# Two transformer blocks with cross attention on one core: weight loads queued one by one, and three value steps moved before the first unit

## The chip, the cores and the metric

The kernel runs on one core of a Trainium2 chip. The metric is the device time of one execution in microseconds (us). The median of three runs of the kernel before is 3282.65 us (3281.64 to 3282.78). The core has a matrix engine (TensorE, PE), a vector engine (VectorE, DVE), a scalar engine (ScalarE, ACT), a general engine (GpSimd, POOL) and a synchronising engine (SyncE, SP), which here issues nearly all DMA transfers.[...]

## The reference

Two layers of the same form are applied to `x` (4 batch items, 512 rows, 320 columns, float32). Each layer has self attention, cross attention to a context of 1601 rows and 192 columns, and a gated feed-forward part; 20 heads of 16 columns.

```python
def _attn(x, ctx, wq, wk, wv, wo, bo, heads):
    q, k, v = ...            # x @ wq, ctx @ wk, ctx @ wv, split into heads
    sim = jnp.einsum('bhid,bhjd->bhij', q, k) * scale
    a = jax.nn.softmax(sim, axis=-1)
    out = jnp.einsum('bhij,bhjd->bhid', a, v)
    ...
    return out @ wo + bo

h1 = _ln(x, n1_g, n1_b)
x = _attn(h1, h1, q1, k1, v1, o1_w, o1_b, heads) + x
h2 = _ln(x, n2_g, n2_b)
x = _attn(h2, context, q2, k2, v2, o2_w, o2_b, heads) + x
h3 = _ln(x, n3_g, n3_b)
proj = h3 @ ff_w1 + ff_b1
a, g = jnp.split(proj, 2, axis=-1)
x = a * jax.nn.gelu(g, approximate=False) @ ff_w2 + ff_b2 + x
```

## The kernel before

**Units.** The work is cut into units (class `Unit`, L206). A self or cross unit is one group of 4 heads of one batch item; there are 5 groups and 4 items, so 20 self units and then 20 cross units per layer. A feed-forward unit is one batch item. The loop at L1179 runs over all units in order. Unit numbers in this document count from 0 within a layer.

**One attention unit** (`main`, L870). The keys are taken in chunks of 128: 4 chunks in a self unit, 13 in a cross unit. For each chunk the scores of the four heads are made on PE (L878), in two half-steps of two heads. ScalarE takes the exponential (L884), and one chunk later the values are summed on PE (L898). From the second chunk on, ScalarE copies the sum (L914) and GpSimd adds it (L915). In a unit that the feed-forward part follows, VectorE does both.

**The maxima.** The exponential needs the maximum of each score row before it starts. So while a unit runs, the full score rows of a later unit are made once more on PE (L717, and L732 for the last 65 keys of a cross unit) and VectorE reduces them (L725). `max_end` (L768) transposes the negated maxima on VectorE (L772) and sends them by eight small DMAs (L779) from the tile `turned` into spare rows of the query tile `q`, where the score matmul subtracts them. It is called for the next unit at the third chunk from the end (L949), in a self unit at the second of four. The next unit's first score waits for those transfers.

**How the maxima are spread.** `giver` (L1094) hands out, at each half-step, one pair of maxima matmuls for the units one and two ahead. Where time presses it adds whole rounds of four ("extra"). Between two extra rounds, one piece of planned work is run if any is ready (L944 to L947).

**The planner.** All other work stands in seven chains (L261): norm, context, projections of queries and keys (`add_proj`, L545), values (`add_values`, L652), division of the sums, output projection (`add_finish`, L784). Each piece has a cost and a due round. A round is one half-step. `pick` (L295) takes the ready piece with the earliest due round; `pace` (L309) works out the cost per round that the due rounds ask for; `tick` adds it to a credit between -2 and 4; `steps` (L331) runs pieces while the credit covers a share of their cost. `until` forces a chain where its result is needed at once. Light pieces (statistics, normalisation, division) run one or two per chunk.

**Queues.** Loads, the small transfers of the maxima, and the transfers `aT<-o` of finished units (L817) are all issued by SP, in the order of the program, and share its queue. Only the eight transfers of unit 0's maxima are divided over SP, ScalarE and GpSimd.

**The start** (L1145 to L1177). The first item of `x` and the first self weights are loaded; the queries and keys of units 0 and 1, the queries of unit 2, the maxima of unit 0 and half of the value steps are worked out; `max_end(first)` sends the maxima. Then the other three items of `x`, the first output weights, the cross weights and the feed-forward weights are loaded in one block (L1170 to L1174), one key projection runs, and the loop over the units begins.

**Later loads.** `after(u)` (L1061) runs when a unit's work on an item is complete. When it is the last item of a part, `after` loads the weights of the same part for the next layer, and the next output weights, at once. For the feed-forward part that is at the start of layer 2's self units.

Of the kernel before, what the change touches and what calls it, by code (L numbers as in the profile page):

```python
# [20 lines left out]
L = 2  # L21
# [38 lines left out]
def kernel(ctx: ExitStack, tc: tile.TileContext, x, context, ws, out):  # L60
# [69 lines left out]


    xs = [const.tile([P, NQ, D], F32, name=f"x{b}") for b in range(B)]

    def load_x(b):
        src = x[b].rearrange("(c p) d -> p c d", p=P)
        for t in range(NQ) if b == 0 else (slice(NQ),):
            dma(out=xs[b][:, t], in_=src[:, t])


    wq1, wk1, wv1, wq2 = (wpool.tile([P, 3, D], F32, name=n) for n in ("wq1", "wk1", "wv1", "wq2"))  # L140
# [8 lines left out]
    brow = [wpool.tile([P, D], F32, name=f"brow{i}") for i in range(2)]  # L149
    lng = [wpool.tile([P, 3], F32, name=f"lng{i}") for i in range(3)]  # L150
    lnb = [wpool.tile([P, 3], F32, name=f"lnb{i}") for i in range(3)]

    def load_rows(t, w, chunks):
        for k, at, n in chunks:
            dma(out=t[:n, k, :], in_=w[at : at + n, :])
# [15 lines left out]
    def load_norm(l, i):  # L171
        for t, v in ((lng[i], ws[l][f"n{i + 1}_g"]), (lnb[i], ws[l][f"n{i + 1}_b"])):
            load_columns(t, v, FK if i == 2 else DK)
            if i == 2:
                for half in range(2):
                    load_columns(t[half * REST :], v, [(2, 2 * P, REST)])
# [7 lines left out]
    def load_out(l, name):  # L184
        load_rows(wo, ws[l][name], DK)

    def load_cross(l):
        load_norm(l, 1)
        load_rows(wq2, ws[l]["q2"], DK)
        load_rows(wk2, ws[l]["k2"], CK)  # L190
        load_rows(wv2, ws[l]["v2"], CK)

    def load_ff(l):
        load_norm(l, 2)
        with nc.allow_non_contiguous_dma(reason="a vector's elements go to partitions"):
            dma(out=b1, in_=ws[l]["ff_b1"].rearrange("(c p) -> p c", p=P))
        load_rows(w1, ws[l]["ff_w1"], FK)
        for half in range(2):
            dma(
                out=w1r[half * REST : (half + 1) * REST, :],  # L200
                in_=ws[l]["ff_w1"][2 * P :, half * FF : (half + 1) * FF],
            )
        dma(out=w2, in_=ws[l]["ff_w2"].rearrange("(c p) f -> p c f", p=P))


    class Unit:  # L206
# [96 lines left out]
    def run(chain):  # L303
        costs, _, ready, _, f = chains[chain].popleft()
        assert ready(), chain
        f()
        clock["credit"] -= sum(costs)
# [80 lines left out]
    def add_norm(l, b, i, put, done, due):  # L388
        xb = xs[b]
        s = {}  # L390

        def stats(t):
            if t == 0:
                hn_used.append(b)
                s["mv"] = two.tile([P, NQ, 2], F32, tag="mv", name="mv")
            st = three.tile([P, 6], F32, tag="st6", name="st6")
            nc.vector.bn_stats(st, xb[:, t, :])
            nc.vector.bn_aggr(s["mv"][:, t, :], st)

        def root():  # L400
            s["rstd"] = inverse_root(s["mv"][:, :, 1])
            s["round"] = clock["round"]

        def normalise(t):
            if t == 0:
                s["hn"] = one.tile([P, NQ, D + REST], F32, tag="hn", name="hn")

            for to, at, n in ((0, 0, D), (D, D - REST, REST))[: 1 + i // 2]:
                nc.vector.tensor_scalar(
                    s["hn"][:, t, to : to + n], xb[:, t, at : at + n],  # L410
                    s["mv"][:, t, 0:1], s["rstd"][:, t : t + 1], ALU.subtract, ALU.mult,
                )
            s["round"] = clock["round"]

        def turn(k, at, n):
            if k == 0:
                s["hT"] = two.tile([P, 3, N], F32, tag="hT", name="hT")
                readers.append(done)
            ps = step_bank([P, N], "hps")
            n += REST if n == REST else 0  # L420
            for t in range(NQ):
                nc.tensor.transpose(ps[:n, t * P : (t + 1) * P], s["hn"][:, t, at : at + n], ident)  # L422
            if start["on"] and k == 1:
                nc.vector.tensor_scalar(
                    s["hT"][:n, k, :], ps[:n, :],
                    lng[i][:n, k : k + 1], lnb[i][:n, k : k + 1], ALU.mult, ALU.add,
                )
            else:
                nc.scalar.activation(
                    s["hT"][:n, k, :], ps[:n, :], AF.Identity,  # L430
                    bias=lnb[i][:n, k : k + 1], scale=lng[i][:n, k : k + 1],
                )
            for t in ((0,), (1,), (2, 3))[k]:

                nc.gpsimd.tensor_tensor(xb[:, t, :], xb[:, t, :], brow[(3 * l + i) % 2], ALU.add)
            if k == 2:
                hn_used.pop()
                put(s["hT"])

        for t in range(NQ):  # L440
            add(
                "norm", LIGHT, lambda t=t: stats(t), due - 22 + t,
                (lambda: stage[b] == 3 * l + i and not hn_used) if t == 0 else yes,
            )
        add("norm", LIGHT, root, due - 18)
        for t in range(NQ):
            add(
                "norm", LIGHT, lambda t=t: normalise(t), due - 13 + t, yes,
                (lambda: clock["round"] >= s["round"] + 4) if t == 0 else yes,
            )  # L450
        for k, at, n in (DK if i < 2 else FK + [(2, 2 * P, REST)]):
            add(
                "norm", 0.58, lambda k=k, at=at, n=n: turn(k, at, n), due - 6 + 2 * k,
                may_overwrite if k == 0 else yes, lambda: clock["round"] >= s["round"] + 1,
            )
# [312 lines left out]
    def max_end(u):  # L768

        turned = two.tile([P, SLOT], F32, tag="turned", name="turned")  # L770

        nc.vector.transpose(turned, u.nm)  # L772
        for half in range(2):
            slots = u.q[half * GD : (half + 1) * GD, :].rearrange("(j s) n -> s j n", s=SLOT)[AUG[2 * half]]
            for i in range(P // SLOT):
                rows = slice(i * SLOT + half * 2 * NQ, i * SLOT + (half + 1) * 2 * NQ)

                queue = (nc.sync, nc.scalar, nc.gpsimd, nc.sync)[i] if start["on"] else nc.sync
                queue.dma_start(  # L779
                    out=slots.rearrange("j (t r) -> j t r", t=NQ)[:, :, i * SLOT : (i + 1) * SLOT],  # L780
                    in_=turned[rows, :],
                )
# [87 lines left out]
    def main(u, give, nxt):  # L870
# [48 lines left out]
        for c in range(u.nch):  # L919
            extra = []  # L920
            if last:

                round_of(
                    [
                        lambda j=j, ring=ring: score(c, j, *ring)
                        for j, ring in zip(range(HG), ((ps_st, "st"), (ps_m, "m")) * 2)
                    ],
                    [],
                )
                tick()  # L930
            else:
                for odd in range(2):
                    if odd:
                        tick()
                    pair, rounds = give(2 * c + odd)
                    extra += rounds
                    round_of([lambda j=j: score(c, j) for j in ((2, 3) if odd else (0, 1))], pair)
            u.scored = c + 1
            flush()
            late.append(lambda c=c: values(c))  # L940
            steps(None, 1 if extra or c == u.nch - 1 else 2)

            start["quad"] = True
            for i, e in enumerate(extra):  # L944
                if i and next_cost() is not None:
                    run(pick())
                round_of([], e)  # L947
            start["quad"] = False
            if not last and c == u.nch - 3:  # L949
                max_reduce(nxt)  # L950
                max_end(nxt)

# [106 lines left out]
    def after(u):  # L1061

        stage[u.b] += 1
        if u.b == B - 1:
            load_bias(u.l, ("self", "cross", "ff").index(u.kind) + 2)
        if u.b == B - 1 and u.l + 1 < L:
            {"self": load_self, "cross": load_cross, "ff": load_ff}[u.kind](u.l + 1)
        if u.b == B - 1 and u.kind == "self":
            load_out(u.l, "o2_w")
        if u.b == B - 1 and u.kind == "cross" and u.l + 1 < L:  # L1070
            load_out(u.l + 1, "o1_w")

    def left(v):
        return sum(map(len, v.pairs))
# [92 lines left out]
    run("values")  # L1167
    max_reduce(first)
    max_end(first)
    for b in range(1, B):  # L1170
        load_x(b)
    load_out(0, "o1_w")
    load_cross(0)
    load_ff(0)  # L1174
    start["on"] = start["both"] = False
    run("proj")
    clock["credit"] = 0.0  # L1177

    for i, u in enumerate(units):  # L1179
# [42 lines left out]
```

## Time and profile before

| what | value |
|---|---|
| median of 3 runs | 3282.65 us |
| the profiled execution | 3282.7 us |
| its span, first to last instruction | 3280.9 us |
| PE busy | 3225.2 us (98%) |
| DVE, ACT, POOL busy | 2093.1, 2030.4, 1524.9 us |
| mean granted PE clock | 0.995 of full speed |
| DMA, mean over the span | 16 GB/s |
| share of PE in the chain that ended last | 89% |

The profile records one execution. A row of the timeline gives start and length in us, the engine, the line of the kernel, the operation, what is written and read, and in brackets how long the engine stood idle before it and what ended that. "SPq" is SP issuing transfers. The window rows give the busy time of each engine within a stretch, then the granted clock, the mean share of the 16 DMA engines in use and GB/s. The rows that carry the argument stand in the prediction.

### The profile page before, as it was taken

What the parts mean: (1) busy time and instruction counts of PE and PEld (TensorE: products, weight loads), DVE (VectorE), ACT (ScalarE), POOL (GpSimd) and SP (SyncE); (2) the same over time, 40 slices, a digit from 0 to 9 for tenths busy, and PEclk for the clock granted to TensorE, in tenths of its full rate; (3) what the DMA queues carried; (4) which work ended last, traced back from release to release, by engine and by line L of the source; (5) the groups of instructions that cost most, each with busy time, mean ns of one, the idle gap of its engine ahead of it and who ended that gap; (6) DMA issues with size and microseconds to landing.
All of it is one profiled execution on the core that took longest, in us unless ns stands there. A gap on an engine that the chain in (4) does not pass through costs nothing.

```text
span 3280.9 us, 82097 instructions
## 1 busy us (share of the span) xinstructions
PE 3225.2 (98%) x33554; PEld 1454.8 (44%) x33554; DVE 2093.1 (64%) x3844; ACT 2030.4 (62%) x4191; POOL 1524.9 (46%) x2254
## 2 busy tenths in 40 slices
PE   7999999999999999999999999999999999999999
PEld 3444444444444444355444444443444444443555
DVE  5777767777777776522247777677777777774221
ACT  3666567877877877711136665678778778775110
POOL 3545455655655655210224554556556556542000
PEclk9999999999999999999999999999999999999999
DMA  4001001100100000000020100000000000000000
GB/s 129 10 21 28 7 7 32 30 8 5 30 10 6 28 5 4 19 6 0 1 65 9 26 9 9 12 7 18 6 19 5 5 19 5 5 5 4 9 10 14
DMA packets 48813, 53.18 MB, mean 16 GB/s; under 512 B 23340, under 2 KB 41780, under 8 KB 47156
## 3 DMA queue, kind: packets, MB, share of 16 engines
q1 hardware_dynamic: 48352, 47.92, 5.5%
q8 instruction: 265, 4.34, 0.5%
q14 instruction: 112, 0.92, 0.1%
q0 software_dynamic: 64, 0.00, 0.0%
q10 hardware_dynamic: 20, 0.00, 0.0%
HBM read 29.21 MB, written 7.54 MB: 11 GB/s over the span
## 4 chain that ended last, share of the span: by engine, by line
PE 89%; DVE 5%; POOL 3%; DMA 1%; issue 1%; ACT 1%; SPq 0%; DVEq 0%; POOLq 0%; ACTq 0%
PE st L878 22%; PE av L898 19%; PE sps L717 14%; PE fps L999 9%; PE yps L1034 5%; PE kps L613 4%; PE vps L665 4%; PE ops L826 3%; PE qps L588 3%; DVE nmax L725 2%; PE fps L1011 2%; PE sps L732 1%; PE hps L422 1%; DVE pm L725 1%; POOL kT L543 1%
## 5 line engine op out<-in xcount | busy, mean ns | idle before, releaser
L884 ACT ACTIVATE pr<-st 128x512 f32<-128x512 f32 (+1 forms) x2720 | 1411.5, 602 | 556.0 <-PE sps L717 425.3
L725 DVE TENSOR_REDUCE pm<-sps 128x1 f32<-128x512 f32 x1920 | 1195.6, 683 | 417.3 <-PE sps L717 414.6
L878 PE MATMUL st<-q,kT 32*128 32x512 f32 (+1 forms) x5440 | 1371.9, 618 | 35.1 <-DMA q<-turned 18.5
L717 PE MATMUL sps<-kT,q 32*128 32x512 f32 x5120 | 1281.9, 620 | 3.8 <-ACT kst L630 2.5
L915 POOL TENSOR_TENSOR o<-o,vo 128x512 f32<-128x512 f32 x576 | 735.4, 1277 | 1059.1 <-ACT vo L914 904.0
L898 PE MATMUL av<-pr,vals 128*32 128x512 f32 (+1 forms) x5440 | 733.0, 607 | 4.2 <-ACT pr L884 4.2
L878 PEld LDWEIGHTS st<-q,kT 32*128 32x128 f32 (+1 forms) x5440 | 468.4, 181 | 347.6 <-ACT pr L884 161.9
L717 PEld LDWEIGHTS sps<-kT,q 32*128 32x128 f32 x5120 | 441.6, 184 | 229.9 <-issue 151.6
L725 DVE TENSOR_REDUCE nmax<-sps 128x1 f32<-128x512 f32 x640 | 396.1, 680 | 149.9 <-PE sps L717 148.1
L543 POOL TENSOR_SCALAR kT<-kst,keep,ones 64x200 f32<-64x200 f32 (+2 forms) x796 | 413.6, 520 | 80.9 <-ACT kst L623 22.3
L914 ACT COPY vo<-av 128x512 f32<-128x512 f32 x576 | 349.5, 607 | 20.4 <-PE av L898 19.7
L898 PEld LDWEIGHTS av<-pr,vals 128*32 128x32 f32 (+1 forms) x5440 | 110.1, 108 | 502.6 <-ACT pr L884 480.3
L999 PE MATMUL fps<-hT,w 128*128 128x512 f32 x640 | 288.0, 599 | 0.0
L1017 ACT ACTIVATE gl<-fps,b 128x512 f32<-128x512 f32 x80 | 54.8, 687 | 376.8 <-PE fps L1011 376.8
L543 POOL TENSOR_SCALAR q<-qst,keep,zero 64x128 f32<-64x128 f32 (+1 forms) x476 | 229.8, 483 | 89.7 <-ACT qst L600 57.9
L999 PEld LDWEIGHTS fps<-hT,w 128*128 128x128 f32 x640 | 117.4, 190 | 147.6 <-issue 142.2
L665 PEld LDWEIGHTS vps<-wv,ctxT 96*32 96x32 f32 (+1 forms) x3264 | 102.8, 109 | 108.0 <-issue 88.8
L665 PE MATMUL vps<-wv,ctxT 96*32 96x192 f32 (+2 forms) x3264 | 148.2, 299 | 0.0
L370 POOL TENSOR_SCALAR root<-root 128x4 f32<-128x4 f32 x23 | 5.3, 229 | 298.6 <-DVE root L364 297.9
L613 PE MATMUL kps<-ctxT,wk 96*32 96x200 f32 (+1 forms) x2560 | 135.9, 332 | 0.0
L1018 DVE SCALAR_TENSOR_TENSOR hid<-fps,b,gl 128x512 f32<-128x512 f32 x48 | 35.8, 750 | 152.2 <-ACT gl L1017 149.9
L588 PE MATMUL qps<-hT,wq 112*32 112x128 f32 (+3 forms) x2880 | 127.5, 309 | 4.1 <-DVE nmax L725 2.5
(79 smaller groups left out, 2245.4 us busy)
## 6 DMA issues: line engine op xcount, KB each, us to landing
aT<-o SPq DMA_DIRECT2D x320, 32.0 KB
q<-turned SPq DMA_DIRECT2D x636, 1.0 KB
ctxT<-ctxT SPq DMA_DIRECT2D x8, 1200.8 KB
w<-in_L_xattn_ff_w_dram SPq DMA_DIRECT2D x4, 1280.0 KB
ctxin<-in_ctx_dram SPq DMA_DIRECT2D x24, 192.0 KB
w<-in_L_xattn_ff_w_dram SPq DMA_DIRECT2D x2, 1600.0 KB
out_dram<-x SPq DMA_DIRECT2D x16, 160.0 KB
x<-in_x_dram SPq DMA_DIRECT2D x3, 640.0 KB
```

The lines of the kernel that those rows point to most:

```text
L543: nc.gpsimd.tensor_scalar(to, stage[rows, :w], keep[b][rows], more[rows], ALU.mult, ALU.add)
L588: nc.tensor.matmul(ps[to, :w], lhsT=wq[:n, k, gs], rhs=first.hT[:n, k, at[i] : at[i] + w], start=(k == 0), stop=(k == 2),)
L613: nc.tensor.matmul(ps[to, :w], lhsT=wk[:n, k, gs], rhs=first.kvT[:n, k, c0 : c0 + w], start=(k == 0), stop=(k == len(u.kck) - 1),)
L665: nc.tensor.matmul(ps[f : f + m, at : at + w], lhsT=u.kvT[:n, k, c * P + f : c * P + f + m], rhs=wv[:n, k, h0 * DH : h1 * DH], start=(k == 0),
L717: nc.tensor.matmul(ps, lhsT=u.q[j * SLOT : (j + 1) * SLOT, t * P : (t + 1) * P], rhs=u.kT[j * SLOT : (j + 1) * SLOT, u.k0 + s * 512 : u.k0 ...
L725: return lambda: nc.vector.tensor_reduce(to, ps, AX.X, ALU.max, negate=(ns == 1))
L878: nc.tensor.matmul(st[:r, :], lhsT=u.kT[rows, u.k0 + c * P : u.k0 + c * P + r], rhs=u.q[rows, :], start=True, stop=True)
L884: nc.scalar.activation(p[:r], st[:r], AF.Exp)
L898: nc.tensor.matmul(ps[i * SLOT : (i + 1) * SLOT, :], lhsT=columns_of[:r, head : head + SLOT], rhs=pr.pop((c, j))[:r, :], start=True, stop= ...
L914: nc.scalar.copy(vo, ps)
L915: nc.gpsimd.tensor_tensor(u.o, u.o, vo, ALU.add)
L999: nc.tensor.matmul(ps, lhsT=w1[:, k, i * FF + c * P : i * FF + (c + 1) * P], rhs=u.hT[:, k, :], start=(k == 0), stop=False,)
```

## The change

1. **A queue of loads.** A deque `loads` is added. The block at the start keeps only `load_x(1)`; the other loads are appended to `loads`, and so are the loads that `after` made (self, cross, feed-forward and output weights), in a somewhat different order. The bias row is still loaded at once.
2. **One load per unit.** In `main`, behind `max_end(nxt)`, the first entry of `loads` is taken and issued. Units that a feed-forward unit follows take none, and feed-forward units take none.
3. **Finer pieces.** `load_ff` no longer loads; it appends five entries: the small vectors with `w1r`, the two 128-row parts of `w1`, and two halves of `w2`.
4. **Conditions on the norm.** `load_x` notes the round. The first statistics of a norm wait until its item has been loaded and, for items other than the first, 5 rounds have passed.
5. **Three value steps.** After the last key projection of the start, `run("values")` is called three times before the credit is set to 0 and the loop begins.

```diff
+    loaded = {}
     def load_x(b):
...
+        loaded[b] = clock["round"]
+    loads = deque()
     def load_ff(l):
-        load_norm(l, 2)
-        with nc.allow_non_contiguous_dma(reason="a vector's elements go to partitions"):
-            dma(out=b1, in_=ws[l]["ff_b1"].rearrange("(c p) -> p c", p=P))
-        load_rows(w1, ws[l]["ff_w1"], FK)
-        for half in range(2):
-            dma(
-                out=w1r[half * REST : (half + 1) * REST, :],
-                in_=ws[l]["ff_w1"][2 * P :, half * FF : (half + 1) * FF],
-            )
-        dma(out=w2, in_=ws[l]["ff_w2"].rearrange("(c p) f -> p c f", p=P))
+        def small():
+            load_norm(l, 2)
+            with nc.allow_non_contiguous_dma(reason="a vector's elements go to partitions"):
+                dma(out=b1, in_=ws[l]["ff_b1"].rearrange("(c p) -> p c", p=P))
+            for half in range(2):
+                dma(
+                    out=w1r[half * REST : (half + 1) * REST, :],
+                    in_=ws[l]["ff_w1"][2 * P :, half * FF : (half + 1) * FF],
+                )
+
+        loads.append(small)
+        for k in FK:
+            loads.append(lambda k=k: load_rows(w1, ws[l]["ff_w1"], [k]))
+        second = ws[l]["ff_w2"].rearrange("(c p) f -> p c f", p=P)
+        for c in (slice(0, NHC // 2), slice(NHC // 2, NHC)):
+            loads.append(lambda c=c: dma(out=w2[:, c], in_=second[:, c]))
...
                 "norm", LIGHT, lambda t=t: stats(t), due - 22 + t,
-                (lambda: stage[b] == 3 * l + i and not hn_used) if t == 0 else yes,
+                (lambda: stage[b] == 3 * l + i and not hn_used and b in loaded) if t == 0 else yes,
+                (lambda: b == 0 or clock["round"] >= loaded[b] + 5) if t == 0 else yes,
...
             if not last and c == u.nch - 3:
                 max_reduce(nxt)
                 max_end(nxt)
+                if loads:
+                    loads.popleft()()
...
         if u.b == B - 1:
             load_bias(u.l, ("self", "cross", "ff").index(u.kind) + 2)
-        if u.b == B - 1 and u.l + 1 < L:
-            {"self": load_self, "cross": load_cross, "ff": load_ff}[u.kind](u.l + 1)
-        if u.b == B - 1 and u.kind == "self":
-            load_out(u.l, "o2_w")
-        if u.b == B - 1 and u.kind == "cross" and u.l + 1 < L:
-            load_out(u.l + 1, "o1_w")
+            if u.kind == "self":
+                loads.append(lambda: load_out(u.l, "o2_w"))
+            if u.kind == "cross" and u.l + 1 < L:
+                loads.append(lambda: load_out(u.l + 1, "o1_w"))
+            if u.l + 1 < L:
+                if u.kind == "ff":
+                    load_ff(u.l + 1)
+                else:
+                    load = load_self if u.kind == "self" else load_cross
+                    loads.append(lambda: load(u.l + 1))
...
-    for b in range(1, B):
-        load_x(b)
-    load_out(0, "o1_w")
-    load_cross(0)
+    load_x(1)
+    loads.append(lambda: load_x(2))
+    loads.append(lambda: load_out(0, "o1_w"))
+    loads.append(lambda: load_x(3))
+    loads.append(lambda: load_cross(0))
     load_ff(0)
     start["on"] = start["both"] = False
     run("proj")
+
+    for _ in range(3):
+        run("values")
     clock["credit"] = 0.0
```

## The prediction

> **What bounds the kernel now.** I read the page first: TensorE is busy 98% of the span and carries 89% of the chain that ended last, so only its idle time and its slow clock can be won. PE's waits, ranked over the span (engine, line, waited for, us, times, longest):
>
> ```profile
> PE st L878 <- DMA q<-turned: 18.5, 5, 9.8
> PE st L878 <- ACT pr L884: 7.0, 7, 1.4
> PE st L878 <- DVE pm L725: 5.0, 8, 0.7
> ```
>
> The largest wait is a score matmul (L878) waiting for the row of maxima that `max_end` (L768) sends into the query tile. PE in order of time (start, length, what, idle before it) shows where:
>
> ```profile
> 27.29 1.48 PE L613 MATMUL kps<-hT,wk 112*32 112x256 f32 x24
> 31.68 0.70 PE L878 MATMUL st<-q,kT 32*128 32x512 f32 x2 [2.92 <-DMA q<-turned]
> ...
> 57.03 1.48 PE L588 MATMUL qps<-hT,wq 112*32 112x256 f32 x24
> 68.27 3.59 PE L878 MATMUL st<-q,kT 32*128 32x512 f32 x8 [9.75 <-DMA q<-turned]
> ...
> 1699.34 1.13 PE L878 MATMUL st<-q,kT 32*128 32x512 f32 x4
> 1701.92 2.07 PE L878 MATMUL st<-q,kT 32*128 32x512 f32 x4 [1.45 <-DMA q<-turned]
> ```
>
> 2.92 us is the latency of the first unit's maxima, 9.75 us that of unit 1's, 1.45 us that of unit 1 of the second layer; 2.26 and 2.15 us more fall at 2457 and 2693 us, behind a context tile. SyncE and VectorE in order of time tell why:
>
> ```profile
> 49.39 2.58 SPq L155 DMA_DIRECT2D w<-in_L_xattn_ff_w_dram  x2
> 52.02 1.23 SPq L199 DMA_DIRECT2D w1r<-in_L_xattn_ff_w_dram  x2
> 53.29 0.59 SPq L203 DMA_DIRECT2D w<-in_L_xattn_ff_w_dram  x1
> 54.05 28.16 SPq L779 DMA_DIRECT2D q<-turned  x16
> ...
> 98.14 4.59 SPq L779 DMA_DIRECT2D q<-turned  x8
> ```
>
> ```profile
> 52.02 0.20 DVE L772 STREAM_TRANSPOSE turned<-nmax 128x32 f32<-128x32 f32 x1
> ```
>
> The maxima of unit 1 are ready at 52.22, but SP issues loads until 53.88, and the eight small transfers stand on the queue behind 4.8 MB of feed-forward weights. The chain lets them land at 59.89 + 8.25 = 68.14. In the second layer it gives the w2 load 17.01 us from 1683.27, and the maxima land 1.49 us after it. Undisturbed, eight issues take 4.45 us and the last lands 1.7 us later (the tile's issues), about 6.2 us after the transpose.
>
> The clock, from 2 us windows (window; PE, PEld, DVE, ACT, POOL busy; clock; DMA):
>
> ```profile
> 34.00:36.00 2.00, 2.00 (x24) 0.99 (x24) 1.56 (x4) 1.08 (x2) 0.00 (x0) 0.50 1.07 386
> 70.00:72.00 2.00, 2.00 (x10) 0.48 (x12) 0.00 (x0) 1.23 (x3) 0.00 (x0) 0.50 0.00 0
> 1704.00:1706.00 2.00, 2.00 (x12) 0.52 (x16) 0.00 (x0) 1.12 (x3) 0.00 (x0) 0.50 0.00 0
> ```
>
> Each of the three gaps is followed by half clock: from the windows at their edges 32.84 to 36.28, 63.56 to 73.8 (busy from 68.27) and 1701.96 to 1708.8 us. A score of eight took 3.59 us there instead of 1.14.
>
> **What the Trainium skill says.** "TensorE: Matmul & The Clock Gate", Part 1: the array's clock halves after an idle window of about 3.4 us and comes back after a busy one. The trace agrees in kind: half clock lasted 3.4, 10.2 and 6.8 us; that 1.45 us of idle set it off shows that less than a whole window can be enough. "DMA: Bandwidth & Descriptors", Queues, rings and completion order: SP owns one ring on each of the 16 engines, and an engine takes its descriptors in ring order; hence small transfers behind large ones are late, as the 8.25 us against 1.7 us show. "Perfetto Trace Analysis", Per-engine timelines (Tensor Engine Instruction): a matmul's end is an estimate of the profiler, so I count in starts.
>
> **The change part by part.**
>
> *Three value steps in the first gap.* They are those of the second half of `add_values` (192 columns), which ran at 34.51 (2.02 us, half clock), 42.10 and 44.26 (1.11 us each). They now follow the key projection that ends at 28.76: 28.76 + 3 x 1.11 = 32.09 us instead of the score's start at 31.68. So 0.41 us is lost there and 2.92 us filled, and the clock should hold. Their banks: VectorE has read the last maxima at 28.24, ScalarE the queries at 27.34 and the values at 27.80; their three copies (0.32 us each) follow the key copy at 30.31 to 30.68, before the first exponential at 32.84. No wait comes of it.
>
> *What they leave behind.* In unit 0 they separated rounds of maxima, in which VectorE is the pace: 12 reductions from 44.35 with 0.62 us each are 7.5 us, against 4 us of PE. Without them nothing stands between the rounds (the projections of unit 3 need unit 0's scores done), and PE waits instead. So unit 0 doesn't lose their whole 3.3 us. I take its length from its twin in layer 2, which runs the same rounds at full clock: first score 1675.23, transpose 1692.92, unit 1's first score 1699.34, that is 17.69 and 6.42 us. From the 17.69 I take 0.9 us: two normalisations of 0.44 on VectorE that won't stand there, since the statistics of the second batch item now wait for round 5. (In before they took 0.66 us each at 35.87 and 42.56.)
>
> *The planner's credit.* Worked through by hand with `pace` (L309): the fourth value step still runs after the first chunk; credit then grows to its limit of 4 by round 8, where before the forced value steps had pushed it to -2, so after the last chunk both queries (57.03) and keys (73.50 before) of unit 3 run. That puts 1.41 us more of useful PE work ahead of unit 1's scores. From round 20 both orders agree again (the second item's normalised rows are turned at round 20 in both).
>
> *The loads.* Unit 1's maxima find SP empty: transpose at 32.1 + 17.7 - 0.9 = 48.9, landed at 48.9 + 0.2 + 6.2 = 55.3. PE reaches unit 1 at 48.9 + 6.4 + 1.4 = 56.7, so the gap closes with 1.4 us to spare. (Without the key projection it would just be covered: 55.3 both.) Unit 1's first chunk then takes 2.8 us (the next one, from 75.06 to 77.86), and its second begins at 59.5 instead of 75.06: **15.5 us** gained, of which 12.7 is idle and the rest clock.
>
> *Layer 2.* The 4.8 MB issued from 1674.92 are spread too. Transpose 1692.92 + 0.2 + 6.2 = 1699.3, just when PE comes. Gained: 1.45 us of idle and half of the 6.83 us at half clock, 4.9; I take **4.5**, since exponentials take 0.6 us each at any clock.
>
> *Where the loads now stand.* Nine come behind the maxima of units 0 to 8 (one issue, 3, 1, 13, 11, then 1 each), seven in layer 2, and two in the cross stage, where units are 50 us long. SP is free between 105.28 and 116.06 and again from 123.06 to 132.64; 13 issues at 0.53 (four took 2.12 us at 1674.92) are 6.9 us, which fits. Behind them wait only the four `aT` issues of the unit before. The most pressing are unit 4's (155.59 to 158.04; first use of them on PE 164.64): behind half of w1, 1.28 MB or 3.5 us at the 364 to 410 GB/s of the windows from 36 to 58 us, they land before 162. Price 0; if that cover is gone, up to 1.5 us once per layer. The next maxima come 17 us after a load. Splitting w1 and w2 adds one issue of 0.5 us. The new conditions on the norms hold nothing later on: x2 and x3 come in units 0 and 2, their norms are added in units 4 and 9; `wo` comes in unit 1 and is read after unit 4.
>
> Sum: 15.5 + 4.5 = 20.0 us. The profiled execution took 3282.7 us (span 3280.9 and 1.8 around it), 0.05 off the median: 3282.7 - 20.0 = **3262.7 us**. Unknown are the wait of PE in unit 0 (plus or minus 1), the ScalarE share (1), POOL's slots for unit 3 coming late (0 to 1 us), and the clock.
>
> **Rivals.**
>
> *The clock halves elsewhere.* In unit 0's second chunk PE now works 4 us in 8. Half clock there costs up to 3.4 us, and layer 2 might keep its half clock (3.4): together 3269.5, range 3267 to 3274. For it: 1.45 us of idle was enough at 1701.9. Against: gaps of 1.4, 2.26 and 2.15 us at 240, 2457 and 2693 passed without.
>
> *More is won.* Half clock also falls at 432 and 2064 us without a large gap before it. A shift of 15 us moves these against the clock's windows; if they go, 3 us each: 3256.7. Against: the three runs lie within 1.1 us, as if it didn't depend on chance.
>
> *Only a move.* VectorE or the latency of 6.2 us, not the loads, holds units 1 and 2, and what is won at 58 is lost by 100: 3279. Against: VectorE idles 16.06 us before 75.82, and unit 1 has no rows of its own left to reduce.
>
> *Slower.* The order of the planner doesn't rejoin: with other credits the projections run at the last moment, and each next unit waits on GpSimd's slots (four of q and four of kT, 5 us: 86.07 to 91.34). It decides from four units on (20 us); ten units give 3282.7 - 20 + 50 = 3313. The same holds if a load were to push every next row of maxima by 3 us. For it: at 150.15 and 240.60 PE waited 0.96 and 1.40 us after such a projection. Against: the rounds worked out above.
>
> **How the numbers follow.** Forecast as above 0.60 (3259.5 to 3266.5); clock elsewhere 0.18; more won 0.11; only a move 0.05; slower 0.06. The range 3256 to 3272 takes in the first and third and most of the second. Within 0.2% (6.6 us, about what a measurement here can tell from no change) is the fourth case: faster 0.89, same 0.05, slower 0.06.
>
> **What would show it.** The waits of L878 for q<-turned fall from 18.5 us to about 4.5, those at 2457 and 2693; value steps stand between 28.8 and 32.1; unit 3's queries and keys both precede unit 1's scores; the clock is 1.00 from 31 to 75 and around 1705; the eight small issues at 49 take 4.5 us and nothing of w1 comes before 130. A PE wait on q<-turned over 2 us in units 1 to 9, or on GpSimd's kT, would make it wrong.

## The result and the profile after

The changed kernel takes 3267.73 us (median of 6 runs, 3265.23 to 3271.09) against 3282.68 us before (6 runs, 3280.94 to 3287.16): ratio 0.9954, 95% interval 0.9942 to 0.9967. That is 15 us or 0.46% faster where 20 us were forecast. The profiled execution is the slowest of the six: 3271.09 us, span 3269.3 us. The views below are its own.

PE's waits of the changed kernel, largest first (engine, line, waited for, us, times, longest; L878 is now L891):

```profile
PE st L891 <- ACT pr L897: 6.9, 7, 1.4
PE cps L514 <- DMA ctxin<-in_ctx_dram: 5.5, 1, 5.5
PE st L891 <- DMA q<-turned: 5.2, 4, 2.0
```

The wait for the maxima fell from 18.5 to 5.2 us. A wait that the kernel before did not have stands in second place: 5.5 us for a piece of the context. PE in order of time (start, length, idle before in brackets):

```profile
28.86 3.12 PE L678 MATMUL vps<-wv,hT 112*32 112x192 f32 x72
32.98 0.70 PE L891 MATMUL st<-q,kT 32*128 32x512 f32 x2 [1.00 <-DMA q<-turned]
...
41.84 6.18 PE L730 MATMUL sps<-kT,q 32*128 32x512 f32 x25
...
55.19 1.48 PE L601 MATMUL qps<-hT,wq 112*32 112x256 f32 x24
56.49 1.48 PE L626 MATMUL kps<-hT,wk 112*32 112x256 f32 x24
57.90 1.14 PE L891 MATMUL st<-q,kT 32*128 32x512 f32 x8
...
584.54 1.92 PE L514 MATMUL cps<-ident,ctxin 128*96 128x128 f32 x8 [5.50 <-DMA ctxin<-in_ctx_dram]
...
1693.15 1.14 PE L891 MATMUL st<-q,kT 32*128 32x512 f32 x8
```

The three value steps fill the first gap but for 1.00 us, unit 3's queries and keys both stand ahead of unit 1's scores, and those begin at 57.90 without a wait (68.27 before). At 1693.15 the wait of layer 2 is gone too. SP in order of time:

```profile
50.52 4.36 SPq L792 DMA_DIRECT2D q<-turned  x8
54.92 0.40 SPq L138 DMA_DIRECT2D x<-in_x_dram  x1
...
569.53 4.45 SPq L792 DMA_DIRECT2D q<-turned  x8
574.02 1.34 SPq L166 DMA_DIRECT2D lng<-in_L_xattn_n_g_dram  x3
575.40 1.47 SPq L166 DMA_DIRECT2D lnb<-in_L_xattn_n_b_dram  x3
576.91 1.36 SPq L161 DMA_DIRECT2D wq<-in_L_xattn_q_dram  x3
578.32 1.36 SPq L161 DMA_DIRECT2D wk<-in_L_xattn_k_dram  x3
579.73 1.36 SPq L161 DMA_DIRECT2D wv<-in_L_xattn_v_dram  x3
581.22 5.64 SPq L480 DMA_DIRECT2D ctxin<-in_ctx_dram  x4
```

At 50.52 the eight small transfers leave at once. At 569.53 the maxima of a cross unit are followed by the 15 issues of layer 2's self weights (7.1 us), and only then come the context pieces that PE transposes at 584.54. Windows of 2 us (PE, PEld, DVE, ACT, POOL busy; clock; DMA share; GB/s), where a clock of 0.50 is what is called half clock here:

```profile
228.00:230.00 2.00, 2.00 (x16) 0.59 (x12) 1.83 (x4) 0.28 (x1) 0.00 (x0) 0.50 0.01 2
584.00:586.00 2.00, 1.46 (x7) 1.43 (x8) 0.00 (x0) 0.36 (x1) 0.00 (x0) 0.50 0.06 21
70.00:72.00 2.00, 1.86 (x36) 1.06 (x36) 2.00 (x5) 0.96 (x3) 1.01 (x1) 1.00 0.35 86
1704.00:1706.00 2.00, 2.00 (x16) 0.47 (x16) 1.35 (x3) 2.00 (x5) 0.13 (x1) 1.00 0.06 1
```

The half clock at 70 and 1704 us is gone. It now stands behind the new wait, and at 228 us behind a pause of 1.36 us that the kernel before has too (1.40 us before 240.60, without half clock behind it).

**Where the time went.** All kernels run the same 2720 exponentials in the same order. The lead below is the start of one exponential in the profile before minus its start in another profile, both counted from the first instruction, so it shows stage by stage what was won; a number that stays from row to row means that nothing was won or lost there. The columns are the changed kernel and five of the experiments, one profile each.

| time before, us | place | changed | self weights at once | values only | loads only | loads, credit 2 | context behind |
|---|---|---|---|---|---|---|---|
| 32.8 | first exponential | -1.3 | -1.3 | -0.9 | -0.3 | -0.2 | -1.5 |
| 76.2 | unit 1, second chunk | 14.4 | 14.3 | 1.4 | 13.8 | 11.9 | 14.1 |
| 97.3 | unit 2 | 15.0 | 15.0 | 0.5 | 8.1 | 12.5 | 14.7 |
| 231.8 | unit 10 | 15.4 | 15.4 | 1.0 | 8.1 | 12.8 | 15.1 |
| 276.9 | unit 12 | 12.2 | 13.8 | 1.0 | 8.2 | 12.8 | 13.4 |
| 440.8 | end of self, layer 1 | 13.5 | 16.7 | 1.0 | 11.2 | 15.6 | 13.2 |
| 540.0 | cross unit 21 | 13.5 | 16.7 | 1.0 | 11.2 | 15.6 | 13.2 |
| 666.5 | cross unit 24 | 6.2 | 16.7 | 1.0 | 2.2 | 6.6 | 13.2 |
| 1697.7 | layer 2, unit 0 | 6.2 | 16.7 | 1.0 | 2.2 | 6.4 | 13.0 |
| 1710.7 | layer 2, unit 1 | 11.3 | 21.8 | 0.6 | 7.3 | 11.5 | 18.1 |
| 2071.8 | end of self, layer 2 | 11.2 | 24.9 | 0.7 | 10.3 | 14.1 | 20.7 |
| 2997.1 | last exponential | 11.4 | 24.3 | -2.3 | 5.1 | 13.6 | 24.8 |

The changed kernel wins 15.0 us by unit 2 and 5.1 us in layer 2, 20.1 us in all. It loses 7.4 us between cross units 21 and 24, and 3.2 us to half clock at 226.5 us; 1.3 us come back where half clock at the end of self attention lasted 3.4 us and not 6.8.

### The profile page after: what moved, and what is told of

It is laid out like the page before. It is cut to its first block, busy times and chain, and to the rows that moved or that the text cites. A ratio compares the mean times of both kernels' runs of the same rounds, so it can differ in the third digit from the quotient of the medians.

```text
span 3269.3 us, 82086 instructions
## 1 busy us (share of the span) xinstructions
PE 3221.7 (99%) x33554; PEld 1455.4 (45%) x33554; DVE 2090.6 (64%) x3844; ACT 2029.1 (62%) x4191; POOL 1525.4 (47%) x2254
## 4 chain that ended last, share of the span: by engine, by line
PE 89%; DVE 5%; POOL 3%; issue 1%; ACT 1%; DMA 1%; SPq 1%; DVEq 0%; POOLq 0%; ACTq 0%
PE st L891 22%; PE av L911 19%; PE sps L730 15%; PE fps L1014 9%; PE yps L1049 5%; PE kps L626 4%; PE vps L678 4%; PE ops L839 3%; PE qps L601 3%; DVE nmax L738 2%; PE fps L1026 2%; PE sps L745 1%; PE hps L434 1%; DVE pm L738 1%; POOL kT L556 1%
## 5 line engine op out<-in xcount | busy, mean ns | idle before, releaser
L891 PE MATMUL st<-q,kT 32*128 32x512 f32 (+1 forms) x5440 | 1368.1, 617 | 21.7 <-ACT pr L897 6.9
L891 PEld LDWEIGHTS st<-q,kT 32*128 32x128 f32 (+1 forms) x5440 | 467.9, 181 | 333.6 <-ACT pr L897 160.4
```

The costliest lines, as they stand in the source:

```text
L891: nc.tensor.matmul(st[:r, :], lhsT=u.kT[rows, u.k0 + c * P : u.k0 + c * P + r], rhs=u.q[rows, :], start=True, stop=True)
```

## The experiments

The kernel before, run beside the experiments, had medians of 3283.6 to 3286.2 us in 7 to 31 runs, up to 4 us over the one above. So two times are compared by their ratios to it, and single us by the traces.

**One load undone.** The changed kernel with layer 2's self weights issued at once in `after`, as before the change.

```diff
                 if u.kind == "ff":
                     load_ff(u.l + 1)
+                elif u.kind == "self":
+                    load_self(u.l + 1)
                 else:
-                    load = load_self if u.kind == "self" else load_cross
-                    loads.append(lambda: load(u.l + 1))
+                    loads.append(lambda: load_cross(u.l + 1))
```

> The changed kernel with one load undone: the self weights of layer 2 (15 issues) are issued at once when the last item of self attention is complete, as in the kernel before; all other loads stay queued. Theory A (the 15 issues behind unit 23's maxima stand on SP in front of the context loads of the next item, and PE waits 5.5 us for the context at 584 us and then works at half clock): that wait is gone (0 to 0.5 us), the distance to the kernel before stays about 15 us from 310 to 1690 us instead of falling from 12 to 6, and the time is 3259 to 3262 us. Rival B (the context comes late because the earlier start moved its tile's turn or the DMA rings are full, not because of SP's order): the wait for the context stays at 4 us or more and the time at 3266 to 3269 us.

Measured: 3263.44 us (3257.81 to 3267.57), ratio to the kernel before 0.9919 (0.9905 to 0.9934), profiled span 3256.4 us. The wait for the context is gone and the lead keeps 16.7 us from 440 to 1700 us. SP of this kernel:

```profile
476.44 1.36 SPq L166 DMA_DIRECT2D lng<-in_L_xattn_n_g_dram  x3
477.85 1.36 SPq L166 DMA_DIRECT2D lnb<-in_L_xattn_n_b_dram  x3
479.26 2.46 SPq L161 DMA_DIRECT2D wq<-in_L_xattn_q_dram  x3
...
566.32 4.45 SPq L792 DMA_DIRECT2D q<-turned  x8
570.89 6.43 SPq L480 DMA_DIRECT2D ctxin<-in_ctx_dram  x4
```

The self weights are issued at 476, two units earlier, and the context pieces follow directly behind the maxima. Theory A holds. The median lies 1.4 us above the forecast, while the kernel before beside it took 3286.24 us; by the ratio 26.6 us are won. The profile, the second fastest of the six runs, had 3.4 us of half clock.

**The dose.** The same 15 issues queued in pieces: 9 and 6, and 6, 3, 3, 3, so that 9 or 6 of them stand in front of the context pieces. The second form, and below it the lines that the first has in place of the three that queue the pieces:

```diff
+                elif u.kind == "self":
+                    n = u.l + 1
+                    loads.append(lambda: load_norm(n, 0))
+                    for t, name in ((wq1, "q1"), (wk1, "k1"), (wv1, "v1")):
+                        loads.append(lambda t=t, name=name: load_rows(t, ws[n][name], DK))
                 else:
-                    load = load_self if u.kind == "self" else load_cross
-                    loads.append(lambda: load(u.l + 1))
+                    loads.append(lambda: load_cross(u.l + 1))
```

```diff
+                    def part():
+                        load_norm(n, 0)
+                        load_rows(wq1, ws[n]["q1"], DK)
+
+                    def rest():
+                        load_rows(wk1, ws[n]["k1"], DK)
+                        load_rows(wv1, ws[n]["v1"], DK)
+
+                    loads.append(part)
+                    loads.append(rest)
```

> The changed kernel with the self weights queued in two pieces of 9 and 6 issues: the middle dose. Theory A: the wait for the context is 5.5 - 6 x 0.47 = 2.7 us (2 to 3.5). Rival B: as with 15 issues, 5 to 6 us.

> The changed kernel with the self weights of layer 2 queued in four pieces (6, 3, 3, 3 issues) in place of one of 15. Theory A (each issue ahead of the context loads makes them 0.47 us later, about 1.7 us are covered): the wait for the context at about 584 us is 5.5 - 9 x 0.47 = 1.3 us (0.5 to 2), without half clock behind it, and between 540 and 670 us no more than 2 us are lost to the kernel before; time 3259 to 3264 us. Rival B (any load behind unit 23's maxima delays the context, whatever its size, through the rings): 4 us or more.

The wait at the same matmul, first with 9 issues in front, then with 6:

```profile
576.41 1.92 PE L514 MATMUL cps<-ident,ctxin 128*96 128x128 f32 x8 [2.15 <-DMA ctxin<-in_ctx_dram]
```

```profile
581.10 1.16 PE L514 MATMUL cps<-ident,ctxin 128*96 128x128 f32 x8 [0.62 <-DMA ctxin<-in_ctx_dram]
```

| issues in front | 0 | 6 | 9 | 15 |
|---|---|---|---|---|
| wait, us | none | 0.62 | 2.15 | 5.50 |

The first context piece is issued 7.46, 8.87 and 11.69 us after the first of the eight small transfers with 6, 9 and 15 issues in front, and 4.57 us after it with none: SP delays it by 0.47 us for each issue in front, as theory A says. PE begins 2.69, 2.79 and 3.33 us after that issue, so the rest of the wait (some 0.1 us with 9, 0.6 us with 15) is a later landing. The bytes of weights in front grow with the issues, and they may be its cause; no run separates the two. Since PE reaches this place 9.5 us after the first small transfer in all three, some 2.3 us of the delay were covered (an estimate, with 2.69 us from a context piece's issue to PE). Rival B falls. With the four pieces the lead lost at this place is 0.9 us in place of 7.4. Its time is 3266.03 us (3258.99 to 3267.01), ratio 0.9939 (0.9924 to 0.9954), above the forecast of 3259 to 3264; its profile had half clock for 6.8 us at 226 and at 420.6, where the other had 3.4 and none. The single run with halves took 3262.43 us.

**The value steps alone.** The kernel before with three `run("values")` behind the last key projection.

```diff
     run("proj")
+
+    for _ in range(3):
+        run("values")
     clock["credit"] = 0.0
```

> The kernel before with the three value steps alone moved into the first gap; the loads stay in their block. Theory A (the loads set when unit 1's maxima land, near 68 us, whatever PE did until then): the first gap shrinks from 2.9 to about 1 us, unit 1's scores still begin at 67 to 69 us behind a wait of 9 us or more, and the time is 3279 to 3283 us. Rival B (the value steps are worth their own 2.9 us of idle and 1.7 us of slow clock in any case): 3277 to 3279 us, with unit 1's scores at 64 us.

Measured: 3282.91 us (3273.8 to 3286.89), ratio 0.9986 (0.9977 to 0.9994).

```profile
32.54 0.70 PE L878 MATMUL st<-q,kT 32*128 32x512 f32 x2 [0.98 <-DMA q<-turned]
...
67.24 3.70 PE L878 MATMUL st<-q,kT 32*128 32x512 f32 x8 [9.71 <-DMA q<-turned]
```

The first gap is filled but for 1 us, and unit 1 still waits 9.7 us for its maxima: the lead is 1.4 us at its second chunk and 1.0 us from unit 10 to layer 2. Rival B's start at 64 us did not come. As theory A has it, time won ahead of a stall that something else ends is only handed on. The times alone don't say so: the ratio is 4.6 us faster, as much as rival B forecast. Four of the 22 runs, with a granted clock of 0.997, took 3274 us, and the others, at 0.993 to 0.995, 3281 to 3287 us; the theory rests on the trace.

**The loads alone**, the changed kernel without the three value steps.

```diff
     run("proj")
 
-    for _ in range(3):
-        run("values")
     clock["credit"] = 0.0
```

> The changed kernel without the three value steps ahead of the first unit; the loads stay queued. Theory A (parts work together: the queue closes the gap of 9.75 us and the half clock behind it, the value steps win about 3 to 4 us in unit 0): first gap 2.9 to 4 us again, no wait over 1 us before unit 1's scores, and 3270 to 3273 us. Rival B (the value steps only move work that VectorE covers in unit 0 anyway): as the changed kernel, 3266 to 3269 us.

Measured: 3277.1 us (3273.1 to 3284.57), ratio 0.9969 (0.9958 to 0.998), 5 us less than the changed kernel's gain, though the two intervals overlap; the profiles differ by 6.2 us in span. At unit 1's second chunk the lead is 13.8 us, nearly the same as with the value steps; 5.8 us of it are lost in the next 10 us:

```profile
64.02 2.07 PE L891 MATMUL st<-q,kT 32*128 32x512 f32 x8
67.63 1.72 PE L730 MATMUL sps<-kT,q 32*128 32x512 f32 x4 [1.54 <-POOL kT L556]
69.28 1.93 PE L911 MATMUL av<-pr,vals 128*32 128x512 f32 x8
```

The keys of unit 3 were projected only behind unit 1's first scores (59.80). GpSimd then took up the chain of the normalisation (62.20 to 65.75) ahead of them, began to write kT only at 65.75, and PE waited; half clock followed from 68.0 to 74.9 us. So the steps are worth more than the gap that they fill.

**Their order without their filling.** The loads alone, with the planner's credit set to 2.0 before the first unit.

```diff
-    for _ in range(3):
-        run("values")
-    clock["credit"] = 0.0
+    clock["credit"] = 2.0
```

> The queued loads without the moved value steps, and the planner's credit set to 2.0 in place of 0 before the first unit. In the run with the loads alone unit 3's keys were projected after unit 1's first scores, PE then waited 1.5 us for GpSimd's kT and half clock followed; the lead on the kernel before fell from 13.8 us (unit 1's second chunk) to 8.1 us (two units later). Theory D (what the value steps bring beyond the first microsecond is their order: with credit left, the keys come ahead of unit 1's scores and GpSimd is in time): with credit alone the keys come ahead too, no wait for GpSimd's kT in units 1 to 3, and the lead stays at 13 to 15 us until 220 us. Rival E (the steps must fill the first gap itself): the lead falls to about 8 us again.

```profile
57.68 1.48 PE L601 MATMUL qps<-hT,wq 112*32 112x256 f32 x24
58.98 1.48 PE L626 MATMUL kps<-hT,wk 112*32 112x256 f32 x24
60.39 1.14 PE L891 MATMUL st<-q,kT 32*128 32x512 f32 x8
```

The keys come ahead of unit 1's scores, no wait for kT follows, and the lead is 11.9, then 12.5 to 12.8 us. Theory D holds in kind: a changed start value of the credit does most of what the steps do beyond the gap. It stays 2.6 us behind the changed kernel, which is about the first gap (2.94 us here, 1.00 there) with 3.4 us of half clock behind it; so the forecast of 13 to 15 was up to 1 us high. Time 3273.69 us (3268.8 to 3275.2), ratio 0.9967 (0.9954 to 0.9979); only the profiles (this one, 3268.80 us, is the fastest of its six runs) show the difference to the loads alone, since the runs scatter by more.

**Layer 2's block.** Three versions of the changed kernel in which the feed-forward weights are issued in one block when layer 1 ends: in the new pieces (`w1r`, `w1`, two halves of `w2`), exactly as before (`w1`, `w1r`, all of `w2`), and as before with `w2` in halves. The first, and then the third (the second has the one load of `w2` in place of the last three lines):

```diff
                 if u.kind == "ff":
+                    held_back = list(loads)
+                    loads.clear()
                     load_ff(u.l + 1)
+                    while loads:
+                        loads.popleft()()
+                    loads.extend(held_back)
```

```diff
                 if u.kind == "ff":
-                    load_ff(u.l + 1)
+                    n = u.l + 1
+                    load_norm(n, 2)
...
+                    load_rows(w1, ws[n]["ff_w1"], FK)
+                    for half in range(2):
+                        dma(
+                            out=w1r[half * REST : (half + 1) * REST, :],
+                            in_=ws[n]["ff_w1"][2 * P :, half * FF : (half + 1) * FF],
+                        )
+                    second = ws[n]["ff_w2"].rearrange("(c p) f -> p c f", p=P)
+                    for c in (slice(0, NHC // 2), slice(NHC // 2, NHC)):
+                        dma(out=w2[:, c], in_=second[:, c])
```

> The changed kernel with one load undone: layer 2's feed-forward weights are issued in one block when the last feed-forward unit of layer 1 is complete, as in the kernel before. Theory A (that block alone caused the wait of 1.45 us and the half clock behind it at 1702 us): a wait of L891 for q<-turned of 1 to 2 us comes back some 6 us after unit 1's transpose in layer 2, and the time is 4 to 5 us above the changed kernel, 3270 to 3274 us. Rival B (the gain of 5 us there comes from elsewhere, a shifted clock window): no such wait and 3266 to 3269 us.

> The changed kernel with layer 2's feed-forward weights issued at once and exactly as in the kernel before: w1 ahead of w1r, and w2 in one transfer of 1.6 MB in place of two halves. Theory C, formed on the run in which the block was at once but in the new pieces (no wait there, 0.2 us lost): the wait at 1702 us was made by the tail of the one large w2 transfer, on whose landing the issue of the last small transfer waits; then a wait of L891 for q<-turned of 1 to 2.3 us comes back and 4 to 6 us are lost between unit 1's first and second chunk. Rival A (the standing block alone matters, and its absence in that run was luck): no wait again, under 1 us lost.

> The changed kernel with layer 2's feed-forward block at once, w1 ahead of w1r as before, and only w2 in two halves. Theory C (the tail of the single w2 transfer makes the wait): as the run with the block in the new pieces, the lead on the kernel before grows by 4.8 to 5.1 us at unit 1's first chunk of layer 2. Rival F (the order of w1 and w1r makes it): as the run with the block exactly as before, the lead grows by 3.5 us or less.

| block | lead won at unit 1, us | the eight small issues, us |
|---|---|---|
| none (changed kernel) | 5.1 | 4.35 |
| new pieces | 4.9 | 5.93 |
| as before | 3.5 | 7.27 |
| as before, w2 in halves | 1.6 | 7.63 |
| (kernel before) | 0 | 7.53 |

Here my theory A failed: the block in the new pieces costs 0.2 us, although it is issued at the same place. Theory C, the tail of the one large transfer, failed too. Exactly as before, the wait came back (1.22 us), but 1.6 us were lost and not 4 to 6; and halving `w2` without changing the order took nothing off it. Rival F is right: only the order of `w1r` and `w1` sets the fourth row of the table apart from the second. Each row is a single profile.

With `w1r` first its slow part (in windows of 1 us the DMA moved 230 to 290 GB/s while it ran, and 350 to 430 later) lies under the issuing of the rest; with `w1r` in the middle the rate falls to between 160 and 260 GB/s halfway. Counted from the transpose of unit 1's maxima, the last packet of `w2` ends at 5.27 us with the new pieces, and at 6.63, 6.99 (in halves) and 6.88 us (kernel before) with the old order. In all four the eighth small issue leaves SP 0.5 us behind that packet. So SP holds the last small transfer until the block has landed; why it does is not shown. The wait on PE stands at the same place in both old forms, the third one's being

```profile
1693.97 1.13 PE L891 MATMUL st<-q,kT 32*128 32x512 f32 x4
1696.63 1.13 PE L891 MATMUL st<-q,kT 32*128 32x512 f32 x4 [1.53 <-ACT pr L897]
```

The profile names ScalarE, but it is the maxima of the second pair of heads: these scores begin 1.59 us behind the eighth small issue, 1.64 us in the second version and 1.62 us in the kernel before, where the profile names the maxima. Half clock decides the rest: it lasted 6.8 us behind this wait in the kernel before, 3.4 us in the third version, and did not come in the second, and the leads won are 0, 1.6 and 3.5 us. The time of the new pieces is 3269.87 us (3266.7 to 3274.91), ratio 0.9941 (0.9928 to 0.9955), no different from the changed kernel; the single runs of the others took 3278.41 and 3275.8 us.

**The context tile behind the maxima.** The self weights at once, and the context tile of layer 2, which stood in front of the maxima at 2198, 2433 and 2669 us, issued behind them.

```diff
         if l:
-            add("context", 0.0, load, due - 14, free)
-            add("context", 0.0, lambda: put(s["cT"]), due - 2, yes, lambda: clock["round"] >= s["round"] + 8)
+            def defer():
+                if clock["sent"]:
+                    load()
+                else:
+                    first_loads.append(load)
...
+            add("context", 0.0, defer, due - 14, free)
+            add("context", 0.0, give_out, due - 2, yes, lambda: "cT" in s and clock["round"] >= s["round"] + 8)
             return
...
                 max_end(nxt)
+                clock["sent"] = True
+                for f in first_loads:
+                    f()
+                first_loads.clear()
                 if loads:
                     loads.popleft()()
```

> The kernel with the self weights at once, and further layer 2's context tile (1.2 MB) issued behind the maxima of the same unit in place of ahead of them. The waits of L891 for q<-turned of 0.4, 2.4 and 2.2 us near 2198, 2433 and 2669 us go; nothing else moves if the tile is still in time (it lands about 5 to 7 us later), so 4 to 5 us are won on the kernel with the self weights at once: span about 3252 to 3258 us with as much half clock. Rival: the tile comes late for its first use and PE waits for it instead, 3 us or more each time.

Measured: 3257.61 us (3257.23 to 3259.22), ratio 0.9919 (0.9903 to 0.9936), below the changed kernel's interval. SP, first with the self weights at once alone and then with the tile behind the maxima:

```profile
2424.91 0.33 SPq L496 DMA_DIRECT2D ctxT<-ctxT  x1
2425.35 7.71 SPq L792 DMA_DIRECT2D q<-turned  x8
```

```profile
2428.32 4.46 SPq L803 DMA_DIRECT2D q<-turned  x8
2432.88 0.34 SPq L497 DMA_DIRECT2D ctxT<-ctxT  x1
```

In the first, PE waited 2.36 us for these maxima at 2433.07. In the second, no wait of the scores for the maxima is left in layer 2, none for the context appeared, and the lead grows by 4.1 us from 2072 us to the end, where that of the self weights at once falls by 0.6. As ratios to the kernel before the two can't be told apart; that the order wins 4.7 us is read from the traces.

## Why the prediction was right or wrong

The direction was right and the time lay within the range, 5 us above the forecast. It fell where the rival of a clock that halves elsewhere had put it (3267 to 3274), but mostly for another reason, the wait for the context. Step by step:

- **The first gap and unit 0.** Right within 1 us. The three steps ran from 28.86; the scores began 0.9 us later than worked out (32.98), since PE waited 1.00 us for the maxima. Unit 0's transpose came at 50.19 and not 48.9, the second chunk being paced by VectorE as said (12 reductions in 7.26 us, PE's rounds in one row of 6.18 us). A score of eight that took 3.59 us before is not the clock alone: single matmuls took 1.06 us and not 0.59, and the eight ran two at a time.
- **The planner's credit.** Right: queries and keys of unit 3 ahead of unit 1's scores. That this was worth several us by itself (the wait for GpSimd's kT) had been priced only as 1.4 us of useful work.
- **The loads of layer 1.** Right: unit 1's second chunk was forecast 15.5 us earlier; 14.4 us were measured there and 15.0 by unit 2.
- **Layer 2.** The size was right, 5.1 us against 4.5, and so were its terms: the wait, 1.2 to 1.5 us with the old order, and half clock for the rest. But the spreading of "The 4.8 MB issued from 1674.92" was not needed for it: with `w1r` first, the block at once keeps 4.9 of the 5.1 us. Whether spreading alone, in the old order, does as much was not run.
- **Where the loads now stand.** This is the step that failed: "two in the cross stage, where units are 50 us long" was priced at 0 with only `aT` behind it. The long unit doesn't help, since the next item's context pieces stand right behind the maxima on SP. The true price of the 15 issues is 5.5 us of wait and half clock after it: 7.4 us in the profile, 8.1 to 9.0 in the other profiles with 15 issues. The sum with it is 20.0 - 7.4 = 12.6 us; the profiled run shows 11.6, the median 15. That the median still lies 5 us from the forecast is in part luck, since half clock differs from run to run: the profiled run had a granted clock of 0.996, the lowest of the six, and the two at 0.998 took 3266.04 and 3266.43 us. (Unit 4's `aT` is first used at 164.46, not 164.64; nothing hangs on it.)
- **The clock.** The rival that the clock halves elsewhere was half right. In the changed kernel's profile neither of its two places had half clock; unit 0's second chunk (46 us) had it in the profiles of four of the variants. At 226 us it came in seven profiles, the changed kernel's too, and cost 1.6 to 3.2 us each time.
- **More is won.** This rival was right in part. Of the half clock at 432 and 2064 us the changed kernel's profile keeps 3.4 us and 6.8 us; with the self weights at once neither is there, and the lead grows by 3.0 us at each.
- **Only a move.** It did not come: the lead is 15.0 us at unit 2 and 15.4 us at unit 10.
- **The slower rivals** did not come: no load pushed a later row of maxima in units 1 to 9, and the orders rejoined.

## What to carry to other kernels

A load that is moved out of one queue's way is moved into another's: list what stands behind its new place on the same issuing engine, in every stage where it may fall, and count 0.5 us for each issue (0.47 us here). Prefer many small pieces, each behind the urgent transfer of its unit, and the slow pieces of a block first. And remove the stall that ends last, then its partners: here the filled gap was worth 1 us without the loads, and the loads lost 6 us without the order that the steps brought.

## What the runs showed of the hardware that I had not expected

**Half clock falls on a grid, and the place of a pause in it can decide.** In every profile all changes of the granted clock lie on one grid of 3.413 us, whose phase against the first instruction differs from run to run (2.1 us before, 1.3 changed, 3.2 loads alone, and so on). All twelve profiles have the same pause of 1.36 to 1.42 us before the same score in unit 10 (at 240.60 us before, 225.13 changed). In seven of them half clock follows: there the pause begins between 0.2 us ahead of a grid line and 1.3 us behind one. In the five others it begins 1.55 to 2.7 us behind one. So at this place the phase tells the two cases apart without overlap, and the length of the pause does not. It is no rule for other places: in the kernel before, the pause of 1.45 us ahead of 1701.92 begins 1.9 us behind a line, and half clock followed.

The Trainium skill has the grid: "TensorE: Matmul & The Clock Gate", Part 1, states a free-running window of 3413 ns that does not start with the kernel, and the profiles agree: every change lies on it. What it does not lead one to expect is that a pause of less than half a window can be enough.

Much of the scatter between runs goes with this. Half clock lasted 3.4 us in the profile with the self weights at once, 34 us before and 44 us with the values only. Of the 31 runs of the kernel before, the five with a granted clock of 0.992 took 3290.2 to 3294.6 us and the eight at 0.995 took 3281.0 to 3283.3 us; the values only took 3273.8 to 3274.6 us in four runs at 0.997 and 3283.1 to 3286.9 us in six at 0.993.

**One fetch of instructions beside the small transfers.** In all nine profiles with the value steps ahead of unit 0, the GpSimd pair of the first maxima landed 2.2 to 3.1 us after its issue, and in the three without them (before, loads alone, loads with credit) after 1.7 to 1.8 us. In each of the nine a transfer of the queue for instructions fell between 27 and 33 us, in the three none. That the two are cause and effect was not tested. The 1.00 us that was left of the first gap ended with this landing: the first of the pair landed at 32.94, and PE began at 32.98.
